# Two graph attention layers on one core: another order of the norm, the reciprocal and the row dots in layer 0

## The chip, the core and the metric

The kernel runs on one core of a Trainium2 chip. The core has a matrix engine (TensorE, PE in the profile, with its weight loads as PEld), a vector engine (VectorE, DVE), a scalar engine (ScalarE, ACT), GpSimd (POOL, which here issues the gathers and scatters) and SyncE (SP, which issues plain transfers). Each engine works through its own queue of instructions and waits on semaphores that other engines raise. Data lie in HBM, in the on-chip SBUF (128 partitions) and in PSUM, which PE writes. The metric is device microseconds of one execution: the median of several timed runs, beside one execution under the profiler.

## What is computed

Two layers over 2708 nodes with 1024 features, and a sparse adjacency matrix (at most 40 neighbours a node). Each layer is an attention over the neighbours, a residual and a norm over the features. The change touches layer 0:

```python
def _L0_gnn_ref(x, adj, Wf, bf, Wg, bg, W, bW):
    f = x @ Wf + bf
    g = x @ Wg + bg
    e = jax.nn.relu(f @ g.T)
    scores = jnp.where(adj > 0, e, NEG)
    attention = jax.nn.softmax(scores, axis=1)
    x_W = x @ W + bW
    return attention @ x_W
...
x = _layernorm(x + _L0_gnn_ref(...), axis=-1)
x = _layernorm(x + _L1_gnn_ref(...), axis=-1)
```

`_layernorm` subtracts the mean and divides by the root of the variance plus 1e-5. Layer 1 has scores `leaky_relu(f1 + f2.T)` with two vectors f1 and f2, one number per node each.

## The kernel before

First the adjacency rows are turned into lists of up to 40 neighbours, and nodes are sorted by degree into 85 groups of 32. Four groups make a block of 128 rows (block 0 has one group). A tile is one gather of 128 rows of x: four neighbours for each of the 32 nodes of a group. The blocks of layer 0 have 20 tiles, but for the first two (15 and 3) and the last three (16, 16, 15).

The weights are joined beforehand: M = Wf Wgᵀ, so the score of node n with neighbour m is x[n] M x[m] plus a term q. Layer 0's loop `for k, u in enumerate(units)` has 22 steps, in the order of blocks 1, 0, 2, 3 and so on. Every step holds work of several blocks at once:

- `lay.sums` (PE): the sums of block u, with weights st on the rows gathered in `ring` (20 slots). It also makes `totals`, the softmax denominators, by small matmuls into a PSUM tile pt. As its matmuls finish, slots become free, and POOL issues the next gathers into them. DVE takes the reciprocal ri of the totals, and ACT writes y, the scaled sums.
- `x_turn` (PE, ACT): transposes of the block two steps ahead, xb to xT, through two pt tiles (the pool ps_t has two buffers, which totals, q_spread and y's transposes share).
- `product(.., Wt, 1)`: the block behind times W, into a pm tile (the pool ps_m has two buffers). `f_product`: the block ahead times M, also into a pm tile. `turn(y..)` transposes y for the next step.
- `replicate(b, r)` (ACT): copies group r of F, 32 rows of pm, four times into the 128 partitions of Fr[b, r]. Four such copies are one replica.
- `dots` (DVE): for each tile of the next block, one fused multiply and sum of ring rows with Fr over 1024 features, into one column of scores. The tiles of groups 0 and 1 come first, alternating, then those of 2 and 3.
- `soft` (DVE, one Exp on ACT): the softmax over the block's scores; it makes st for the next step's sums, and last the row sums rs.
- `close(back)`, a generator: adds the residual z (gathered by `load_residual`) to the product in pm, runs `norm`, writes X1S for layer 1, computes two row dots with u2b and u1b (f2 and f1 of layer 1), and scatters z with the dots into table T1. The tile zs is the only buffer of z.
- `q_dot`, `q_spread`: the q term of a block, one dot over xb and a small matmul.
- `load_x`, `load_lists`: POOL's gathers of xb and of four parts of the neighbour lists SL.

`norm` is bn_stats and bn_aggr on DVE, then a root by an integer first guess and three Newton turns of three instructions each, then one Identity on ACT with scale and bias. Both layers use it.

All five engines are wrapped in `InOrder`, so each engine's instructions run in the order in which the Python code issues them. Nearly all show line 71, that of the wrapper, in the profile, so groups are told apart by their tiles. The order on DVE in one step of the loop is: add, bn_stats, root and sh of `close`; q dot; the row dots; ri; the dots; q; softmax. On ACT it is: Exp, y's transposes copied, replica 0, Identity on z, replicas 1 and 2, y, xT, replica 3. On POOL: ring gathers, scatter into T1, xb, z, four list gathers.

Of the kernel before, what the change touches and what calls it, by code (L numbers as in the profile page):

```python
# [8 lines left out]
F32 = mybir.dt.float32  # L9
BF16 = mybir.dt.bfloat16  # L10
I32 = mybir.dt.int32
AF = mybir.ActivationFunctionType
ALU = mybir.AluOpType
# [5 lines left out]
EPS = 1e-5  # L19
# [87 lines left out]
def listed_path(ctx, tc, x, adj, Wf, bf, Wg, bg, W, bW, W1, a1, a2, out):  # L107
# [491 lines left out]
    def scatter(table, idx, src):  # L599
        pool.indirect_dma_start(  # L600
            out=table, out_offset=bass.IndirectOffsetOnAxis(ap=idx, axis=0), in_=src,
            in_offset=None, bounds_check=N - 1, oob_is_err=False)

    def norm(z, n, made=None):


        st = small.tile([P, H, 6], F32, name="bst")
        mv = small.tile([P, 2], F32, name="mv")
        for h in range(H):
            if made is not None:  # L610
                made(h)
            dve.bn_stats(st[:n, h, :], z[:n, h * 512:(h + 1) * 512])
        dve.bn_aggr(mv[:n], st[:n])
        var, r, t = (small.tile([P, 1], F32, name=s) for s in ("var", "rstd", "newton"))
        dve.tensor_scalar(var[:n], mv[:n, 1:2], EPS, None, op0=ALU.add)
        ri, ti = r.bitcast(I32), t.bitcast(I32)
        dve.tensor_scalar(ti[:n], var.bitcast(I32)[:n], 1, None, op0=ALU.logical_shift_right)
        dve.tensor_scalar(ri[:n], ti[:n], -1.0, float(0x5F3759DF), op0=ALU.mult, op1=ALU.add)
        for _ in range(3):
            dve.tensor_scalar(t[:n], var[:n], r[:n], r[:n], op0=ALU.mult, op1=ALU.mult)  # L620
            dve.tensor_scalar(t[:n], t[:n], -0.5, 1.5, op0=ALU.mult, op1=ALU.add)
            dve.tensor_scalar(r[:n], r[:n], t[:n], None, op0=ALU.mult)
        sh = small.tile([P, 1], F32, name="sh")
        dve.tensor_scalar(sh[:n], mv[:n, 0:1], r[:n], -1.0, op0=ALU.mult, op1=ALU.mult)
        yield
        act.activation(z[:n, :D], z[:n, :D], AF.Identity, bias=sh[:n], scale=r[:n])
# [24 lines left out]
    class Layer:  # L651
# [57 lines left out]
            u.rs = small.tile([P, Q], F32, name="rs")  # L709
            dve.tensor_reduce(u.rs[:, :u.G], sc, AX.X, ALU.add)  # L710

        def sums(self, u, po, y):

            place = lambda k, h: 32 * ((k + 2 * h) % 4)

            def totals():
                pt = ps_t.tile([P, 4, P], F32, name="pt")  # L720
                for h in range(H):
                    for k in range(u.G):
                        j = place(k, h)
                        pe.matmul(pt[j:j + 32, 0, h:h + 1], stack, u.rs[:, k:k + 1], start=True, stop=True)
                return pt

            index = {(k, t): m for m, (k, g, t) in enumerate(u.tiles)}

            queues = []
            for c in range(4):  # L730
                two = [(k, h) for h, k in enumerate((c, (c + 2) % 4)) if k < u.G]
                if c > 1:
                    two.reverse()
                queues.append([(k, h, t) for t in range(u.T) for k, h in two if t < TILES[u.gs[k]]])
            done, halves, pt = 0, {}, None
            while any(queues):
                if pt is None and done >= min(4, u.T):
                    pt = totals()
                now = [q.pop(0) for q in queues if q]
                for k, h, t in now:  # L740
                    j = place(k, h)
                    pe.matmul(po[j:j + 32, h, :], u.st[:, u.col[k, t], :],
                              self.rows(u.at + index[k, t])[:, h * 512:(h + 1) * 512],
                              start=(t == 0), stop=(t == TILES[u.gs[k]] - 1))
                for k, h, t in now:
                    halves[k, t] = halves.get((k, t), 0) + 1
                    if halves[k, t] == H:
                        self.free.add(u.at + index[k, t])
                        self.gathers()
                        done += 1  # L750
            if pt is None:
                pt = totals()
            ri = small.tile([P, H], F32, name="ri")
            spans = [(slice(0, P), slice(0, H))] if u.G == 4 else \
                [(slice(j, j + 32), slice(h, h + 1)) for h in range(H) for j in (place(0, h),)]
            for rows, h in spans:
                dve.reciprocal(ri[rows, h], pt[rows, 0, h])
            for h in range(H):
                rows = slice(0, P) if u.G == 4 else slice(place(0, h), place(0, h) + 32)
                c = slice(h * 512, (h + 1) * 512)  # L760
                act.activation(y[rows, c], po[rows, h, :], AF.Copy, scale=ri[rows, h:h + 1])
# [95 lines left out]
    def load_lists(b):  # L857
        for g in groups[b]:
            gather(pool, SL[:, g, :], LD[:, :], idq[:, g:g + 1], N * Q)
# [9 lines left out]
    with ExitStack() as s0s:  # L869
# [10 lines left out]
        def load_x(b):  # L880
            xb[b] = xp.tile([P, D], F32, name="xb") if b > 0 else zs[:, :D]
            gather(pool, xb[b][:nrows[b]], x, ids[:nrows[b], b:b + 1])
# [5 lines left out]
        def q_dot(b):  # L888
            n = nrows[b]
            qs = small.tile([P, 1], F32, name="qs")  # L890
            dot(xb[b][:n], rb, n, qs[:n])
            qd[b] = spread(qs[:n], n, "qd")
# [9 lines left out]
        def x_turn(b):  # L902
            xTs[b] = tp.tile([P, KC, P], F32, name="xT")
            for _ in turn(xb[b], nrows[b], xTs[b]):
                pass
# [4 lines left out]
        def replicate(b, k):  # L910

            Fr[b, k] = frp.tile([P, D], F32, name="Fr")
            for p in range(Q):
                act.copy(Fr[b, k][32 * p:32 * p + 32, :], flat(F[b])[32 * k:32 * k + 32, :])

        def dots(u, lo, hi):
            for m in range(lo, hi):
                k, g, t = u.tiles[m]
                dot(lay.rows(u.at + m), Fr[u.b, k], P, u.sc[:, k, t:t + 1])
# [12 lines left out]
        def close(b):  # L932

            n, m, z = nrows[b], valid[b], Z.pop(b)
            pm = Wp.pop(b)

            def add(h):
                c = slice(h * 512, (h + 1) * 512)
                dve.tensor_add(z[:n, c], pm[h][:n, h, :], z[:n, c])

            if b + 1 < NB:
                dve.tensor_add(z[:n, :D], flat(pm)[:n], z[:n, :D])
            steps = norm(z, n, None if b + 1 < NB else add)
            next(steps)
            yield
            for _ in steps:
                pass
            sp.dma_start(X1S[start[b]:start[b] + m, :], z[:m, :D])
            yield
            dot(z[:n, :D], u2b, n, z[:n, D:D + 1])  # L950
            dot(z[:n, :D], u1b, n, f1[:n, b:b + 1])
            yield
            if z is not zs:
                pool.memset(z[:, D + 1:], 0.0)
            scatter(T1[:, :], ids[:m, b:b + 1], z[:m])
# [65 lines left out]
        soft(units[0])  # L1021
        for _ in spread2:
            pass
        closing, loaded = iter(()), 3
        for k, u in enumerate(units):
            nxt = units[k + 1] if k + 1 < len(units) else None
            b = u.b
# [6 lines left out]
            if back is not None:  # L1034
                for _ in yTs[back][1]:
                    pass
            reps = list(range(len(nxt.gs))) if nxt is not None and not first else []
            for r in reps[:1]:
                replicate(nxt.b, r)
            next(closing, None)  # L1040
            if loaded is not None:
                q_dot(loaded)
                loaded = None
            next(closing, None)
            for r in reps[1:3]:
                replicate(nxt.b, r)
            if nxt is None:

                for _ in closing:
                    pass  # L1050
                Wp[back] = product(P, yTs.pop(back)[0], Wt, 1)
            lay.sums(u, po, y[b])
            for _ in closing:
                pass
            closing = iter(())
            if ahead is not None and not first:
                x_turn(ahead)
            if k + 3 < NB and not first:
                loaded = seq[k + 3]
                load_x(loaded)  # L1060
            if back is not None and nxt is not None:
                load_residual(back)
                if back > 0:
                    Wp[back] = product(P, yTs.pop(back)[0], Wt, 1)
                else:
                    Wp[back] = whole(split_product(yTs.pop(back)[0], Wt, frp.tile([P, D], F32, name="Fr"), 1))
# [16 lines left out]
            if k + 2 == NB:  # L1083
                for _ in steps:
                    pass
            if k + 4 < NB and not first:
                load_lists(seq[k + 4])
            if nxt is not None:
                dots(nxt, 0, len(nxt.tiles))
            for _ in spreading:  # L1090
                pass
            if nxt is not None:
                soft(nxt)
            if back is not None:
                closing = close(back)
                next(closing)
# [529 lines left out]
```

## Time and profile before

| What | Value |
|---|---|
| median of 3 timed runs | 1904.17 us (1901.87 to 1906.42) |
| profiled execution | 1750.29 us, span 1748.6 us |
| mean granted PE clock in it | 0.957 |
| PE, DVE, ACT, POOL busy, of the span | 1563.6, 1297.5, 643.5, 1180.9 us |
| same, 0 to 220 us (lists, weights) | 171.5, 171.7, 109.6, 164.9 us |
| same, 220 to 326 us (layer 0, first two blocks) | 89.2, 66.0, 44.5, 67.2 us |
| same, 326 to 977 us (16 steps of layer 0's loop) | 630.0, 594.9, 333.2, 454.8 us |
| same, 977 to 1130 us (layer 0's end) | 138.5, 117.2, 67.9, 65.3 us |
| same, 1130 to 1748.6 us (layer 1) | 534.6, 347.6, 88.3, 428.7 us |

The profile is of one execution; its busy times are sums of instruction durations of one engine. A matmul's end is modelled, so PE's busy time is a rough figure. A wait is named after what released the engine last. The timed runs are executions without the profiler, and their median lies 154 us above the profiled one.

### The profile page before, as it was taken

To read this page: it belongs to the slowest core of one execution; us is meant where nothing else is said; L and a number is where in the kernel's file an instruction comes from. 1 tells how busy PE (TensorE), PEld (TensorE's weight loads), DVE (VectorE), ACT (ScalarE), POOL (GpSimd) and SP (SyncE) were. 2 spreads that over 40 slices of the span, in tenths; PEclk is the share of its full clock that TensorE was granted. 3 is DMA by queue.
4 is the path that set the end of the run, shared out by engine and by line. 5 is a ranking of instruction groups with operands and counts; after the bars stand their busy time and mean duration, and the time that the engine had idled before them with its cause. 6 is when DMAs were issued, how large, how long until landed. Compare 5 with 4: busy or idle time off the path is not lost. (4 is left out here: it accounts for less than half of the span.)

```text
span 1748.6 us, 23112 instructions
## 1 busy us (share of the span) xinstructions
PE 1563.6 (89%) x6969; PEld 675.5 (39%) x6969; DVE 1297.5 (74%) x4262; ACT 643.5 (37%) x902; POOL 1180.9 (68%) x1195
## 2 busy tenths in 40 slices
PE   4999578899999999999999999559899888999896
PEld 2444233344444444444444444213344333343332
DVE  5879846899999989998999977547465555665652
ACT  4555455444444554555554444101111111111111
POOL 7888476467667767776677743177777777777740
PEclk8999778999999999999999999879999999999998
DMA  7656168578877777888887876399999999999960
GB/s 287 228 185 236 38 232 309 199 252 292 302 277 283 269 253 276 294 293 284 303 299 285 291 267 249 121 394 357 367 374 392 391 397 375 384 392 390 396 253 38
DMA packets 149986, 502.80 MB, mean 288 GB/s; under 512 B 32340, under 2 KB 32372, under 8 KB 147144
## 3 DMA queue, kind: packets, MB, share of 16 engines
q0 software_dynamic: 132032, 428.29, 66.2%
q1 hardware_dynamic: 10202, 55.72, 8.4%
q10 hardware_dynamic: 7618, 17.23, 2.7%
q8 instruction: 57, 0.93, 0.2%
q14 instruction: 77, 0.63, 0.1%
HBM read 509.64 MB, written 33.75 MB: 311 GB/s over the span
## 5 line engine op out<-in xcount | busy, mean ns | idle before, releaser
L71 POOL DMA_INDIRECT ring<-in_x_dram,SL x405 | 429.9, 1062 | 164.0 <-issue 70.0
L71 DVE SCALAR_TENSOR_TENSOR j<-ring,Fr 128x1024 bf16<-128x1024 f32 x402 | 493.9, 1229 | 41.1 <-DMA ring<-in_x_dram,SL 13.9
L71 PE MATMUL po<-ring,st 128*32 128x512 f32 x2616 | 324.4, 616 | 56.9 <-ACT y L71 32.5
L71 ACT COPY Fr<-pm 32x1024 f32<-32x1024 f32 (+2 forms) x353 | 340.6, 965 | 18.8 <-PE pm L71 14.1
L71 PE MATMUL pm<-M,yT 128*128 128x512 f32 (+1 forms) x704 | 313.3, 598 | 0.5 <-ACT yT L71 0.5
L71 PE MATMUL pm<-Wt,xT 128*128 128x512 f32 (+1 forms) x704 | 300.5, 599 | 4.7 <-DMA Wt<-in_L_gnn_W_dram 4.7
L71 POOL DMA_INDIRECT ring<-T,SL x249 | 247.0, 992 | 80.5 <-issue 66.3
L71 PE MATMUL pm<-M,xT 128*128 128x512 f32 x672 | 297.5, 601 | 0.0
L71 ACT ACTIVATE scores<-scores 128x12 f32<-128x12 f32 (+9 forms) x65 | 14.0, 216 | 631.6 <-DVE scores L71 631.6
L71 PEld LDWEIGHTS pm<-M,yT 128*128 128x128 f32 (+1 forms) x704 | 127.8, 186 | 185.0 <-issue 183.8
L71 PEld LDWEIGHTS pm<-Wt,xT 128*128 128x128 f32 (+1 forms) x704 | 131.0, 189 | 163.4 <-issue 154.6
L71 PEld LDWEIGHTS pm<-M,xT 128*128 128x128 f32 x672 | 130.2, 194 | 158.0 <-issue 155.1
L71 POOL DMA_INDIRECT more<-T,SL x156 | 154.6, 991 | 48.5 <-issue 43.8
L71 PEld LDWEIGHTS po<-ring,st 128*32 128x32 f32 x2616 | 95.9, 113 | 229.8 <-issue 174.0
L412 POOL TENSOR_TENSOR adj<-adj,iota 128x2708 f32<-128x2708 f32 (+3 forms) x23 | 130.6, 5685 | 22.7 <-ACT adj L71 22.6
L415 DVE MAX8 cand<-adj 128x8 f32<-128x136 f32 (+2 forms) x440 | 97.2, 285 | 37.4 <-POOL adj L412 37.4
L71 PE MATMUL pm<-halfT,WfT 128*128 128x512 f32 x256 | 114.1, 601 | 1.1 <-ACT WfT L71 1.1
L71 POOL DMA_INDIRECT SL<-LD,idq x85 | 86.4, 1016 | 25.8 <-issue 24.0
L71 PE MATMUL po<-more,st 128*32 128x512 f32 x624 | 82.4, 625 | 14.3 <-ACT y L71 14.3
L71 DVE TENSOR_SCALAR scores<-ring,f1q 128x4 f32<-128x4 f32 (+6 forms) x69 | 16.5, 245 | 104.1 <-DMA ring<-T,SL 93.1
L71 POOL DMA_INDIRECT z<-in_x_dram,ids x21 | 24.0, 1142 | 87.1 <-DVE j L71 36.4
L71 PEld LDWEIGHTS pm<-halfT,WfT 128*128 128x128 f32 x256 | 48.2, 193 | 58.0 <-issue 55.2
(214 smaller groups left out, 1539.5 us busy)
## 6 DMA issues: line engine op xcount, KB each, us to landing
adj<-in_adj_dram SPq DMA_DIRECT2D x21, 1354.0 KB, 5.8
X1S<-z SPq DMA_DIRECT2D x19, 512.0 KB, 5.2
ring<-in_x_dram,SL POOLq DMA_INDIRECT x405, 6.5
rows<-in_L_gnn_Wg_dram ACTq DMA_DIRECT2D x8, 512.0 KB, 4.4
rows<-in_L_gnn_Wf_dram ACTq DMA_DIRECT2D x8, 512.0 KB, 3.5
rows<-in_L_gnn_W_dram ACTq DMA_DIRECT2D x8, 512.0 KB, 6.1
Wt<-in_L_gnn_W_dram ACTq DMA_DIRECT2D x1, 4096.0 KB
M<-in_L_gnn_W_dram SPq DMA_DIRECT2D x1, 4096.0 KB
```

Of the source, the lines that this page charges most:

```text
L71: made = self.tc.keep_in_program_order(op(*args, **kwargs))
L412: nc.gpsimd.tensor_tensor(k[:n, cut], k[:n, cut], iota[:n, cut], op=ALU.mult)
L415: nc.vector.max(cand[:n, s, :], k[:n, s * SEG:min((s + 1) * SEG, N)])
```

## The change

In layer 0 `close` no longer calls `norm`, except for the last block. The residual add becomes a fused instruction that also sums the row; the mean is one more small instruction; ACT squares z with the mean as bias and sums (its elementwise output goes into the pm tile, where nobody reads it); the root is a new helper `rsqrt`, with Newton turns of two instructions instead of three, which `norm` uses too, in both layers. The generator has more stops, so that its parts lie elsewhere in the step: the square ahead of replica 0, the root, Identity and the rest inside `sums` by a callback `aside` after the totals. The reciprocal ri is taken right after the totals. Five dots of the next block follow at once, ahead of the two row dots; the last four dots come after q. The q dot moves from after the norm to the end of the step before. The list gathers are issued ahead of the residual gather.

```diff
+    def rsqrt(v, n, scale):
+        half, r, t = (small.tile([P, 1], F32, name=s) for s in ("half", "rstd", "newton"))
+        dve.tensor_scalar(half[:n], v, 0.5 * scale, 0.5 * EPS, op0=ALU.mult, op1=ALU.add)
+        ri, ti = r.bitcast(I32), t.bitcast(I32)
+        dve.tensor_scalar(ti[:n], half.bitcast(I32)[:n], 1, None, op0=ALU.logical_shift_right)
+        dve.tensor_scalar(ri[:n], ti[:n], -1.0, float(0x5F3759DF - 0x400000 - (1 << 31)), op0=ALU.mult, op1=ALU.add)
+        for _ in range(3):
+            dve.tensor_scalar(t[:n], half[:n], r[:n], r[:n], op0=ALU.mult, op1=ALU.mult)
+            dve.tensor_scalar(r[:n], t[:n], 1.5, r[:n], op0=ALU.subtract, op1=ALU.mult)
+        return r
...
-        var, r, t = (small.tile([P, 1], F32, name=s) for s in ("var", "rstd", "newton"))
-        dve.tensor_scalar(var[:n], mv[:n, 1:2], EPS, None, op0=ALU.add)
...
-        for _ in range(3):
-            dve.tensor_scalar(t[:n], var[:n], r[:n], r[:n], op0=ALU.mult, op1=ALU.mult)
-            dve.tensor_scalar(t[:n], t[:n], -0.5, 1.5, op0=ALU.mult, op1=ALU.add)
-            dve.tensor_scalar(r[:n], r[:n], t[:n], None, op0=ALU.mult)
+        r = rsqrt(mv[:n, 1:2], n, 1.0)
...
-        def sums(self, u, po, y):
+        def sums(self, u, po, y, aside):
...
             def totals():
...
-                return pt
+                for rows, h in spans:
+                    dve.reciprocal(ri[rows, h], pt[rows, 0, h])
+                aside()
...
-            for rows, h in spans:
-                dve.reciprocal(ri[rows, h], pt[rows, 0, h])
...
             if b + 1 < NB:
-                dve.tensor_add(z[:n, :D], flat(pm)[:n], z[:n, :D])
-            steps = norm(z, n, None if b + 1 < NB else add)
-            next(steps)
-            yield
-            for _ in steps:
-                pass
+                mean, ss, sh = (small.tile([P, 1], F32, name=s) for s in ("mean", "ss", "sh"))
+                dve.scalar_tensor_tensor(z[:n, :D], flat(pm)[:n], 1.0, z[:n, :D], op0=ALU.mult, op1=ALU.add,
+                                         accum_out=mean[:n])
+                dve.tensor_scalar(mean[:n], mean[:n], -1.0 / D, None, op0=ALU.mult)
+                yield
+                act.activation(flat(pm)[:n], z[:n, :D], AF.Square, bias=mean[:n], accum_out=ss[:n])
+                yield
+                r = rsqrt(ss[:n], n, 1.0 / D)
+                dve.tensor_scalar(sh[:n], mean[:n], r[:n], None, op0=ALU.mult)
+                yield
+                act.activation(z[:n, :D], z[:n, :D], AF.Identity, bias=sh[:n], scale=r[:n])
...
-        closing, loaded = iter(()), 3
+        closing = iter(())
+        q_dot(3)
         for k, u in enumerate(units):
...
+            next(closing, None)
             for r in reps[:1]:
                 replicate(nxt.b, r)
-            next(closing, None)
-            if loaded is not None:
-                q_dot(loaded)
-                loaded = None
-            next(closing, None)
-            for r in reps[1:3]:
-                replicate(nxt.b, r)
...
-            lay.sums(u, po, y[b])
+            def aside():
+                next(closing, None)
+                for r in reps[1:2]:
+                    replicate(nxt.b, r)
+                next(closing, None)
+                for r in reps[2:3]:
+                    replicate(nxt.b, r)
+
+            lay.sums(u, po, y[b], aside)
+            early = 0
+            if nxt is not None and not first:
+                early = min(5, sum(k < 2 for k, _, _ in nxt.tiles))
+                dots(nxt, 0, early)
             for _ in closing:
                 pass
...
                 load_x(loaded)
+            if k + 4 < NB and not first:
+                load_lists(seq[k + 4])
             if back is not None and nxt is not None:
                 load_residual(back)
...
-            if k + 4 < NB and not first:
-                load_lists(seq[k + 4])
             if nxt is not None:
-                dots(nxt, 0, len(nxt.tiles))
+                dots(nxt, early, max(0, len(nxt.tiles) - 4))
             for _ in spreading:
                 pass
             if nxt is not None:
+                dots(nxt, max(0, len(nxt.tiles) - 4), len(nxt.tiles))
                 soft(nxt)
+            if loaded is not None:
+                q_dot(loaded)
+                loaded = None
```

More of the change, by code (lines that the diff above doesn't have):

```diff
@@ L613, in norm @@
         dve.bn_aggr(mv[:n], st[:n])
-        var, r, t = (small.tile([P, 1], F32, name=s) for s in ("var", "rstd", "newton"))
-        dve.tensor_scalar(var[:n], mv[:n, 1:2], EPS, None, op0=ALU.add)
-        ri, ti = r.bitcast(I32), t.bitcast(I32)
-        dve.tensor_scalar(ti[:n], var.bitcast(I32)[:n], 1, None, op0=ALU.logical_shift_right)
-        dve.tensor_scalar(ri[:n], ti[:n], -1.0, float(0x5F3759DF), op0=ALU.mult, op1=ALU.add)
-        for _ in range(3):
-            dve.tensor_scalar(t[:n], var[:n], r[:n], r[:n], op0=ALU.mult, op1=ALU.mult)
-            dve.tensor_scalar(t[:n], t[:n], -0.5, 1.5, op0=ALU.mult, op1=ALU.add)
-            dve.tensor_scalar(r[:n], r[:n], t[:n], None, op0=ALU.mult)
+        r = rsqrt(mv[:n, 1:2], n, 1.0)
         sh = small.tile([P, 1], F32, name="sh")
@@ L710, in soft @@
             dve.tensor_reduce(u.rs[:, :u.G], sc, AX.X, ALU.add)
-        def sums(self, u, po, y):
+        def sums(self, u, po, y, aside):
             place = lambda k, h: 32 * ((k + 2 * h) % 4)
+            ri = small.tile([P, H], F32, name="ri")
             def totals():
@@ L724, in totals @@
                         pe.matmul(pt[j:j + 32, 0, h:h + 1], stack, u.rs[:, k:k + 1], start=True, stop=True)
-                return pt
+                spans = [(slice(0, P), slice(0, H))] if u.G == 4 else \
+                    [(slice(j, j + 32), slice(h, h + 1)) for h in range(H) for j in (place(0, h),)]
+                for rows, h in spans:
+                    dve.reciprocal(ri[rows, h], pt[rows, 0, h])
+                aside()
             index = {(k, t): m for m, (k, g, t) in enumerate(u.tiles)}
@@ L734, in sums @@
                 queues.append([(k, h, t) for t in range(u.T) for k, h in two if t < TILES[u.gs[k]]])
-            done, halves, pt = 0, {}, None
+            done, halves, summed = 0, {}, False
             while any(queues):
-                if pt is None and done >= min(4, u.T):
-                    pt = totals()
+                if not summed and done >= min(4, u.T):
+                    summed = True
+                    totals()
                 now = [q.pop(0) for q in queues if q]
@@ L750, in sums @@
                         done += 1
[L751 to L755, printed above, removed]
-            for rows, h in spans:
-                dve.reciprocal(ri[rows, h], pt[rows, 0, h])
+            if not summed:
+                totals()
             for h in range(H):
@@ L941, in close @@
             if b + 1 < NB:
-                dve.tensor_add(z[:n, :D], flat(pm)[:n], z[:n, :D])
-            steps = norm(z, n, None if b + 1 < NB else add)
-            next(steps)
-            yield
-            for _ in steps:
-                pass
+                mean, ss, sh = (small.tile([P, 1], F32, name=s) for s in ("mean", "ss", "sh"))
[9 more added lines that the diff above has]
+                act.activation(z[:n, :D], z[:n, :D], AF.Identity, bias=sh[:n], scale=r[:n])
+            else:
+                steps = norm(z, n, add)
+                next(steps)
+                yield
+                yield
+                yield
+                for _ in steps:
+                    pass
             sp.dma_start(X1S[start[b]:start[b] + m, :], z[:m, :D])
@@ L1092, in listed_path @@
             if nxt is not None:
+                dots(nxt, max(0, len(nxt.tiles) - 4), len(nxt.tiles))
                 soft(nxt)
+            if loaded is not None:
+                q_dot(loaded)
+                loaded = None
             if back is not None:
```

## The prediction

> **What bounds the kernel now.** I read the stretches first. Between 326 and 977 us, sixteen equal steps of layer 0's loop run; PE is busy 630 of 651 us and DVE 595, all other engines far less. So both are near full, and I asked which waits for which. PE's waits from 300 to 1120 us:
>
> ```profile
> PE pt L71 <- DVE ri L71: 13.7, 14, 3.1
> PE po L71 <- DVE st L71: 5.4, 9, 1.0
> PE pm L71 <- ACT Fr L71: 5.3, 2, 4.1
> ```
>
> (us in total, times, longest.) PE waits for DVE, at two places: the second transpose group of xb waits for the reciprocal ri, and the sums wait for the weights st. Then the timeline of DVE for one step, the one from 609.74 us (start, us, engine, line, operation, idle before):
>
> ```profile
> 609.74 0.17 DVE L71 TENSOR_REDUCE rs<-scores 128x4 f32<-128x24 f32 x1
> 610.33 1.23 DVE L71 TENSOR_TENSOR z<-pm,z 128x1024 f32<-128x1024 f32 x1 [0.42 <-DMA z<-in_x_dram,ids]
> ...
> 615.96 0.21 DVE L71 TENSOR_SCALAR sh<-mv,rstd 128x1 f32<-128x1 f32 x1
> 616.09 1.21 DVE L71 SCALAR_TENSOR_TENSOR j<-xb,rb 128x1024 bf16<-128x1024 f32 x1
> ...
> 617.48 1.22 DVE L71 SCALAR_TENSOR_TENSOR j<-z,u2b 128x1024 bf16<-128x1024 f32 x1
> ...
> 619.90 0.17 DVE L71 RECIPROCAL ri<-pt 128x2 f32<-128x2 f32 x1
> 620.02 1.23 DVE L71 SCALAR_TENSOR_TENSOR j<-ring,Fr 128x1024 bf16<-128x1024 f32 x1
> ...
> 621.55 1.22 DVE L71 SCALAR_TENSOR_TENSOR j<-ring,Fr 128x1024 bf16<-128x1024 f32 x1 [0.30 <-ACT Fr L71]
> ...
> 650.64 0.17 DVE L71 TENSOR_REDUCE rs<-scores 128x4 f32<-128x24 f32 x1
> ```
>
> From rs to rs is 40.90 us. DVE is never idle over 0.8 us in it: norm, q dot, two row dots, ri, twenty dots, softmax. The second dot starts 11.81 us after rs, and waits 0.30 us for ACT's copies of F. And ACT in the same step:
>
> ```profile
> 609.93 4.04 ACT L71 COPY Fr<-pm 32x1024 f32<-32x1024 f32 x4
> 616.20 1.24 ACT L71 ACTIVATE z<-z,sh,rstd 128x1024 f32<-128x1024 f32 x1 [2.23 <-DVE sh L71]
> 617.47 8.13 ACT L71 COPY Fr<-pm 32x1024 f32<-32x1024 f32 x8
> ```
>
> The first replica Fr is copied while DVE computes the norm; the second ends at 621.54, and the second dot starts at 621.55. The replicas are thus only just hidden. All of DVE's norm and row dots (10.2 us) lie in a stretch in which the dots couldn't run anyway.
>
> PE's own floor: steps in which it waits for nothing start their sums at 367.73, 406.94 and 446.25, so 39.2 to 39.3 us. The sixteen steps from 326.40 to 976.85 take 650.45, or 40.65 each. All that could be won from PE's waits there is 16 x 1.4 = 22 us.
>
> **What the Trainium skill says.** "Perfetto Trace Analysis", section "Tensor Engine Instruction (MATMUL, LD_WEIGHTS)": ACT, DVE and GpSimd queues are strict FIFO. The trace agrees: ACT idles 2.23 us ahead of the z instruction while the copies behind it could have run. "ScalarE: Activation LUTs", section "Step-by-step: what each stage is for": writing PSUM is quicker for ScalarE than writing SBUF; no row here has SBUF to PSUM. "TensorE: Matmul & The Clock Gate", section "Part 1: The HAM clock gate": idle PE loses its clock. Here a 3.14 us gap before 1027.44 is followed by a product of 14.72 instead of 13.90 us and transposes and bias row 0.9 us longer: 1.7 us.
>
> **The change part by part**, over DVE's step, T = start of rs. DVE's new order is rs, q dot, add, mean, ri, root, five dots, two row dots, eleven dots, q, four dots, softmax; ACT's is Square, two replicas (8 copies), z, one replica, y, xT, one replica.
>
> 1. q dot, 0.09 to 1.48 (the old start-to-start: 616.09 to 617.48). z's gather has landed by then: it was 0.42 us late against T + 0.6.
> 2. Summing add: 1.26, as a dot row with its accumulator read starts the next; to 2.74. mean 0.15; to 2.89. ri (0.17) and the totals' matmuls, which end 1.8 after T, are done in time. PE's wait for ri goes: -13.7 us of PE.
> 3. Square on ACT: not in the trace. Above: 1.24 like z's Identity (SBUF to SBUF); below: 1.01, the 128x1024 copy out of PSUM. I take 1.24, since the source is SBUF, and add the accumulator read of adj's rows, 0.19. From 2.93 to 4.36.
> 4. Shorter root: three small rows at 0.19 start to start, three pairs of 0.31 + 0.25, sh 0.21: 2.46 us, where the old had 2.8 + 0.2. It starts at 4.40 and ends at 6.86. Bn_stats and its aggregate (1.53) are gone. DVE's work per step falls by some 1.9 us.
> 5. But the replicas stand behind Square in ACT's queue. Eight copies at 8.13: first replica at 8.42, second at 12.49. Tiles alternate between groups 0 and 1, so dot 0 runs at 8.45 and dot 1 at 12.52. DVE idles 1.4 (Square), 1.6 and 2.8 us. Before, dot 1 ran at 11.81.
> 6. After that nineteen dots, 19 x 1.265 = 24.04; the row dots, now behind five dots, 2.54; q 0.14; softmax 3.99 (605.75 to 609.74). 12.52 + 24.04 + 2.54 + 0.14 + 3.99 = 43.23. Before: 11.81 + 24.04 + 0.14 + 3.99 = 39.98, and 0.92 of small ring waits make the 40.90.
>
> So the row dots were free under the replicas, and now they are not; the idle they leave is filled with waiting.
>
> 7. Lists ahead of z: POOL's z gather waited 4.33 us for T's scatter, and four list gathers of 1.30 start to start, 5.2 us, fit there. z is issued some 1 us later at most, hidden by the q dot. Ring gathers start 3 us sooner; 20 x 1.30 from T + 1 keeps ahead of the dots, so the 0.92 of ring waits goes. It is in step 6 already. xb, ahead of the lists, is unmoved and has landed (5.4 us after issue).
> SP's X1S store goes out 6 us later with z (13.7 instead of 7.7 after T); it lands 5.2 later and only the next z gather needs it. T's scatter waits for the row dots, done at T + 20.1; ring gathers hold POOL until T + 27 anyway.
> 8. q four dots earlier frees a PSUM buffer for y's transposes: nothing, PE isn't waiting there.
> 9. pm is held by Square until T + 4.4; PE wants it 10 us after T: nothing. The fourth replica ends at 24.3, PE's F product starts at 25.1: just hidden.
> 10. PE then has 39.25 of work in 43.23, and a gap of 4 us before each sums. By the 1.7 us above, its slower clock takes half of that; DVE still ends last.
> 11. Shorter root in layer 1: 0.56 us for each of 22 blocks on DVE, behind gathers (DMA share 0.91 over that stretch): nothing, but on the two ends, layer 0's last norm and the last norm of all: -1.1.
>
> Sum: 16 x (43.23 - 40.65) = +41.3. The next two steps have 16 tiles: DVE 43.23 - 4 x 1.265 = 38.2, PE bound. They took 39.65 and 42.52 (with the 3.14 wait and its clock). Now 39.25 + 2.0 for the clock, and 42.52 - 3.14 - 1.7 = 37.7: together -3.2. The last step, with PE busy throughout, is equal. +41.3 - 3.2 - 1.1 = +37. Profiled time 1750.29 (span 1748.6): 1787. The median of the runs shown is 154 us above the profile, for which I see no cause in the trace. I take it as constant: 1904 + 37 = 1941.
>
> **Rivals.**
> A. DVE and PE as forecast, but PE's clock in the timed runs is what makes them 154 us longer than the profile. If PE's step is over 43.2 (clock below 39.25 / 43.2 = 0.91 of the profiled one), the longer DVE step is covered. For it: the 154 us; against: the granted clock over 326 to 977 us is 0.99. ri is then early enough either way: no change, 1904.
> B. The other side: faster. Place: DVE's stretch from T to dot 1. If that falls from 12.5 to below 8.5, DVE fits PE's 39.25 and PE's waits of 22 us go: 1904 - 22 - 1 = 1881. It decides from 4 us less, so two replicas would have to be out by the time I have one. For it: ACT is only 51% busy there. Against: the FIFO and the 8.13.
> C. Slower still: PE's gap cools it by more than 4 us, as after 346 us where a 4.08 gap was followed by a product of 15.86, and sums too run slow (9.62 for 7.05 at 328): 2.4 + 2.6 = 5.0, a step of 44.3. 16 x 1.1 = 17 more: 1958.
>
> **How the numbers follow.** Forecast 0.68, A 0.09, B 0.11, C 0.12. The forecast's own range: Square 0.43 shorter (write to PSUM, read hidden) is 7 us less, 0.5 us per step of unseen semaphore time or ri held up by slow totals 8 more, clock after the 16 tile steps 2 either way: 1928 to 1954. The whole range takes in C and stops short of B: 1902 to 1960. A measurement of this kernel tells 0.2%, 3.8 us, from no change. Slower: 0.68 + 0.12 + 0.02 of A; same: 0.07; faster 0.11.
>
> **What would show it.** Right: in the stretch 326 to 1000 DVE's rs recur every 43 us; dot 1 follows rs by 12.5, ended by ACT Fr; waits of DVE on Square near 1.4 each; PE's wait for ri gone and its wait for st up from 5.4 to over 20 us; ring waits of dots near zero; layer 1 equal in length. Wrong: rs every 39 to 40 us, or PE busy throughout (A, B); Square over 2 us; a step set by PE with its products at 15 us or more (C).

## The result, and the profile after

| | before | after |
|---|---|---|
| median of 4 timed runs of one job | 1905.3 us (1901.87 to 1909.23) | 1987.61 us (1975.87 to 2006.42) |
| ratio, 95% interval | | 1.0425 [1.0372, 1.0479] |
| profiled execution (span), clock | 1750.29 us (1748.6), 0.957 | 1975.87 us (1973.8), 0.924 |

By the medians the change costs 82 us where 37 were forecast, and the time lies above the whole range of the forecast, which ended at 1960. The two profiled executions must not be subtracted. Jobs, sets of runs made together, ran on different chips: the kernel before takes 1747 to 1749 us on two of them (profiled there: 1742.6) and 1888 to 1910 on three others (profiled: 1904.3). Which chip the first job's runs had is not on record, but its profile of before fits the quick ones and its median the late ones. So the 154 us between the two lie between chips, and not between runs with and without a profiler. Below they are called quick and late chips, and ratios are taken within one job only. On the late chips the runs of one kernel spread by up to 4%, and the comparisons below leave out those over 1.5% above the fastest of their kernel. Each late chip was met in one job only, so a chip and what else went on at that time can't be told apart.

The traces differ too. Those of quick chips, the first profile of before among them, hold 21,672 to 21,837 semaphore events, those of late chips, the profile after among them, 9,737 to 12,172. What ended a wait is read from these events. So in a trace of a late chip `issue` or `remote` can stand for an event that is missing from it.

DVE's timeline in the profile after, one step (start, us, engine, line, operation, idle before):

```profile
641.05 0.17 DVE L71 TENSOR_REDUCE rs<-scores 128x4 f32<-128x24 f32 x1
...
645.26 0.15 DVE L71 TENSOR_SCALAR half<-ss 128x1 f32<-128x1 f32 x1 [0.82 <-ACT pm L71]
...
649.19 1.23 DVE L71 SCALAR_TENSOR_TENSOR j<-ring,Fr 128x1024 bf16<-128x1024 f32 x1 [1.48 <-issue]
...
653.26 1.23 DVE L71 SCALAR_TENSOR_TENSOR j<-ring,Fr 128x1024 bf16<-128x1024 f32 x1 [2.84 <-issue]
...
681.46 0.22 DVE L71 TENSOR_SCALAR q<-pt,s 128x4 f32<-128x4 f32 x1 [6.34 <-remote]
...
690.30 0.17 DVE L71 TENSOR_REDUCE rs<-scores 128x4 f32<-128x24 f32 x1
```

The first half is as forecast: dot 1, the second of the twenty, starts 12.2 us after rs (forecast 12.52), after DVE idled 0.8, 1.5 and 2.8. The second half is not: DVE stands 6.34 us at q, and the step takes 49.25 us instead of 43.2. ACT in the same step:

```profile
643.98 1.12 ACT L71 ACTIVATE pm<-z,mean 128x1024 f32<-128x1024 f32 x1 [2.61 <-DVE mean L71]
...
645.13 8.09 ACT L71 COPY Fr<-pm 32x1024 f32<-32x1024 f32 x8
653.25 1.24 ACT L71 ACTIVATE z<-z,sh,rstd 128x1024 f32<-128x1024 f32 x1
```

The eight copies run only after Square, as the forecast had it. DVE's waits from 300 to 1330 us (us in total, times, longest us), some left out:

```profile
DVE j L71 <- ACT Fr L71: 55.6, 16, 19.3
DVE q L71 <- remote: 51.8, 9, 8.1
...
DVE ri L71 <- PE po L71: 38.3, 14, 8.6
```

The forecast had nothing for DVE's waits at q and at ri. PE, over the same stretch:

```profile
PE pm L71 <- issue: 44.6, 48, 2.6
PE po L71 <- DVE st L71: 41.0, 13, 5.8
```

PE waits for the weights st, as forecast (5.4 before, "over 20" expected), but it also stands idle 48 times ahead of a matmul into pm, mostly inside its products, without a named releaser; the first profile of before showed none of these. Below they are called holes.

### The profile page after: what moved, and what is told of

The parts are those of the page before. It is cut to its first block, busy times and chain, and to the rows that moved or that the text cites. A ratio compares the mean times of both kernels' runs of the same rounds, so it can differ in the third digit from the quotient of the medians.

```text
span 1973.8 us, 22931 instructions
## 1 busy us (share of the span) xinstructions
PE 1644.7 (83%) x6947; PEld 691.1 (35%) x6969; DVE 1237.4 (63%) x4109; ACT 675.4 (34%) x944; POOL 1167.1 (59%) x1195
## 5 line engine op out<-in xcount | busy, mean ns | idle before, releaser
L71 POOL DMA_INDIRECT ring<-in_x_dram,SL x405 | 417.3, 1030 | 374.2 <-PE po L71 232.4
L71 PE MATMUL po<-ring,st 128*32 128x512 f32 x2616 | 358.6, 652 | 116.5 <-issue 57.2
L71 PE MATMUL pm<-M,xT 128*128 128x512 f32 x672 | 312.4, 618 | 23.7 <-issue 23.7
L71 PE MATMUL pm<-Wt,xT 128*128 128x512 f32 (+1 forms) x704 | 308.4, 601 | 16.4 <-issue 15.1
L71 PE MATMUL pm<-M,yT 128*128 128x512 f32 (+1 forms) x704 | 318.1, 601 | 4.0 <-issue 2.3
L71 PEld LDWEIGHTS po<-ring,st 128*32 128x32 f32 x2616 | 102.0, 118 | 308.1 <-issue 256.6
L71 ACT ACTIVATE y<-po,ri 128x512 f32<-128x512 f32 (+1 forms) x88 | 58.1, 685 | 255.6 <-remote 129.4
L71 PE MATMUL po<-more,st 128*32 128x512 f32 x624 | 98.8, 658 | 21.1 <-issue 20.6
L71 PE MATMUL pt<-ident,y 128*128 128x128 f32 (+1 forms) x352 | 52.7, 273 | 23.4 <-issue 19.7
L71 ACT COPY xT<-pt 128x512 f32<-128x512 f32 (+2 forms) x109 | 48.2, 499 | 63.2 <-PE pt L71 48.0
```

The costliest lines, as they stand in the source:

```text
L71: made = self.tc.keep_in_program_order(op(*args, **kwargs))
```

## Experiments

**1. The two kernels on several chips.** The kernel before is c_before and b2_before, the changed one the other four.

> The kernel before, once more, with its profile taken among the timed runs. Theory 1 (the 154 us between the profiled execution and the timed ones are work that the profile of before didn't show, such as PE slowed or held up): the span of this profile is near 1900 us, with gaps of PE and a clock below 0.957. Theory 2 (a constant outside the span): span near 1749 us again, and a time near 1905.

> The changed kernel once more, on a chip where the kernel before takes about 1747 us. Theory FIFO (DVE's step grows to 43.2 us, by the sum of the prediction): 1747 + 37 = 1784 us, ratio 1.021, rs every 43.2 us from the third to the eighteenth block, PE's records free of holes of a microsecond and more inside a product. Rival (the change is slow by 4% on any chip, since PE's releases come late in it): ratio 1.035 or more, with DVE's q waiting 3 to 8 us for PE as in the first profile.

> The kernel before. If it takes about 1905 us here, its profile shows what the 158 us against 1747 are. Theory L (on such a chip PE's releases reach the others late): DVE's waits for PE are many in it, and records of PE have holes inside products; layer 1, which the change hardly touches, is longer than the 605 us of the run at 1741. Rival (transfers are slower there): DVE's waits are for gathers, and GB/s in layer 1 are lower without holes in PE.

> The changed kernel. Where before takes 1747 us: theory FIFO 1784 us (ratio 1.021) with rs every 43.2 us; rival, that it is slow by 4% anywhere, ratio 1.035 or more. Where before takes 1905 us: 1.04 to 1.05 again.

> The changed kernel. Where before takes about 1747 us: theory FIFO says rs every 43.2 us over sixteen steps and 1784 us (ratio 1.021). Rival (PE is held up by the changed order itself, on any chip): holes of PE without a releaser as on the other chips, steps of 49 us, ratio 1.035 or more. Where before takes about 1900 us: 1.03 to 1.05 as measured before.

> The changed kernel again, to stand beside the other three on one chip. If PE is late here as on the chips of the earlier jobs, 1.03 to 1.05 of before, with steps from rs to rs of 43 us where DVE finds PE's results done and of 49 us where it doesn't. If this is a chip on which before takes about 1750 us, the forecast's sum should hold: +37 us, 1.021, with steps of 43.2 us throughout.

| run | chip | this, us | before in the job, us | ratio |
|---|---|---|---|---|
| before, c | quick | 1747.68 | 1747.09 | 1.0002 [0.9988, 1.0016] |
| after, a4 | quick | 1779.76 | 1749.09 | 1.0188 [1.014, 1.0235] |
| before, b2 | late | 1901.34 | 1887.99 | 1.0068 [1.0008, 1.0128] |
| after, a2 | late (that of b2) | 1947.86 | 1887.99 | 1.0323 [1.0255, 1.0391] |
| after, c | late | 1979.4 (2 runs) | 1900.9 | none given |
| after, a3 | late | 1965.7 (2 runs) | 1901.5 | none given |

On a quick chip the change costs 30.7 us; on the late ones about 60 to 78, and in the result's job 82, or 72 without its longest run. So the chip decides whether the forecast's 37 holds. (The same source as before came out 0.7% off on b2's chip from two runs, so differences below 1% there say little.) The timeline of DVE in a4:

```profile
665.76 0.17 DVE L71 TENSOR_REDUCE rs<-scores 128x4 f32<-128x24 f32 x1
...
673.90 1.23 DVE L71 SCALAR_TENSOR_TENSOR j<-ring,Fr 128x1024 bf16<-128x1024 f32 x1 [1.47 <-ACT Fr L71]
...
677.97 1.23 DVE L71 SCALAR_TENSOR_TENSOR j<-ring,Fr 128x1024 bf16<-128x1024 f32 x1 [2.84 <-ACT Fr L71]
...
699.76 0.21 DVE L71 TENSOR_SCALAR q<-pt,s 128x4 f32<-128x4 f32 x1
...
708.84 0.17 DVE L71 TENSOR_REDUCE rs<-scores 128x4 f32<-128x24 f32 x1
```

43.08 us from rs to rs against 43.23 forecast; no wait at q; and ACT's copies named as the releaser of both dots. All sixteen steps take 42.7 to 43.1. On b2's chip, the stretches of the sixteen steps of before and of after (columns: the stretch and its length; busy us of PE, PEld, DVE, ACT, POOL; granted clock; DMA share; GB/s):

```profile
341.00:1049.00 708.00, 660.50 (x2924) 286.80 (x2924) 597.20 (x1324) 334.24 (x404) 472.89 (x431) 0.97 0.75 260
```

```profile
329.00:1097.00 768.00, 673.15 (x2935) 284.06 (x2937) 568.41 (x1263) 353.63 (x435) 440.09 (x432) 0.93 0.68 240
```

The loop alone is 60 us longer, which is the whole of the difference between these two profiles; PE's recorded work grew by 13 of them, and PE is idle in the rest. In c_before, on a quick chip, the same sixteen steps of before took 653 us, and b2's extra 54 lie in two places. Some 30 are in its first four steps (340.77 to 535.06), over which the granted clock was 0.89, against 0.99 in c_before. The other 24 are in the later twelve, where the clock was 1.00 in both. There the sums differ, while the products are equal and without holes; first b2_before (535.06 to 1048.48), then c_before (483.59 to 972.53); columns: count, busy us, mean ns of one, idle us before:

```profile
L71 PE MATMUL pm<-Wt,xT 128*128 128x512 f32 x384 | 166.8, 592 | 0.0
L71 PE MATMUL po<-ring,st 128*32 128x512 f32 x960 | 129.5, 602 | 19.5 <-DVE st L71 13.0 <-issue 4.3
```

```profile
L71 PE MATMUL pm<-Wt,xT 128*128 128x512 f32 x384 | 166.8, 592 | 0.0
L71 PE MATMUL po<-ring,st 128*32 128x512 f32 x960 | 107.2, 594 | 5.8 <-DVE st L71 5.8
```

In a2 the products have holes, as in the profile after. PE's timeline there, with the product that starts at 590.27:

```profile
589.70 0.28 PE L71 MATMUL pt<-qd,rep 128*128 128x4 f32 x2
...
598.30 0.59 PE L71 MATMUL pm<-M,xT 128*128 128x512 f32 x1 [0.58 <-issue]
600.41 0.59 PE L71 MATMUL pm<-M,xT 128*128 128x512 f32 x1 [1.52 <-issue]
602.51 1.01 PE L71 MATMUL pm<-M,xT 128*128 128x512 f32 x1 [1.51 <-issue]
```

and DVE there:

```profile
604.72 0.22 DVE L71 TENSOR_SCALAR q<-pt,s 128x4 f32<-128x4 f32 x1 [6.30 <-remote]
```

q needs the two matmuls recorded at 589.70, yet is released only at 604.72, 15 us later, and after holes in the product behind them. In the semaphore events of a4 the signal follows the recorded end by 0.01 us (691.47, 691.48); in a2 it comes at 604.69, after an end recorded at 589.98.

**2. The replica ahead of Square.** The forecast's mechanism by itself.

```diff
-            next(closing, None)
             for r in reps[:1]:
                 replicate(nxt.b, r)
+            next(closing, None)
```

> The changed kernel with ACT's Square put behind the first replica instead of ahead of it. Theory FIFO (the replicas held up behind Square set the step): first replica back at T + 4.3, second at T + 9.8 instead of 12.5, so 2.7 us less on each of 16 steps: 1988 - 43 = 1945 us. Rival (PE held up or slowed is what makes the changed kernel slow, whatever ACT's order): within 10 us of 1988.

> The changed kernel with the first replica ahead of Square. It took 1744 us (0.997) where before takes 1747. Where before takes about 1900 us: theory FIFO alone says 40 us less than the changed kernel in the same job; theory L (q ahead of the last four dots waits for a late PE) says q's waits of 46 us or more stay, so it is still slower than before, ratio 1.01 to 1.03.

On a quick chip 0.9971 [0.9944, 0.9998], against 1.0188 for the changed kernel on another: most steps take 40.3 us instead of 42.9. What DVE waits for there, 300 to 1240 us:

```profile
DVE half L71 <- ACT pm L71: 56.3, 21, 3.7
...
DVE j L71 <- ACT Fr L71: 9.2, 19, 0.6
```

The waits for Fr are gone but for 0.5 us each; DVE waits 2.7 us for Square instead, together 3.2 us a step, where a4's step has 0.9, 1.5 and 2.8. This is the strict queue that the Trainium skill states ("Perfetto Trace Analysis", "Tensor Engine Instruction (MATMUL, LD_WEIGHTS)"), with its price measured: two lines swapped in ACT's queue, 2.6 us a step. On a late chip it took 1947 to 1966 us, and the two runs of a3 in the same job 1951 and 1980, so what the swap is worth there isn't resolved. The loss stays: the ratio to before is 1.0274 [1.0182, 1.0367].

**3. bn_stats in place of Square.** Summing add and Square go, the old norm comes back with the shorter root; the rest of the change stays.

```diff
-                act.activation(flat(pm)[:n], z[:n, :D], AF.Square, bias=mean[:n], accum_out=ss[:n])
...
+                dve.tensor_add(z[:n, :D], flat(pm)[:n], z[:n, :D])
+            steps = norm(z, n, None if b + 1 < NB else add)
```

> The changed kernel with the statistics back on DVE (bn_stats and bn_aggr), no Square; all else of the change stays. Theory FIFO: ACT's replicas no longer wait, dots start at T + 6.8 and go on at T + 8.3; the DVE step is about 39.1 us, PE's 39.25 is the bound, faster than before by 16 x 1.4 + 5 = 27 us: 1878 us (ratio 0.986). Rival (the moved row dots and the q ahead of the last four dots cost by themselves): slower than before, 1930 us or more.

> The changed kernel with bn_stats on DVE instead of Square on ACT, as before; it had ratio 0.991 where before takes 1747 us. Where before takes 1905 us: theory FIFO alone would give the same 0.99; theory L adds q's waits, so ratio 1.00 to 1.02.

On a quick chip 0.9906 [0.9881, 0.9931]: dot 1 comes 8.4 us after rs, against 11.7 in c_before. On b2's chip 0.9985 [0.9943, 1.0027], better than either expectation. Its sixteen steps there:

```profile
341.00:1042.00 701.00, 647.63 (x2925) 277.82 (x2924) 589.03 (x1275) 332.75 (x400) 457.94 (x432) 0.96 0.74 262
```

So with DVE busier than in a2 (589 against 568 us) the loop is 67 us shorter. And although q and ri keep their early places, DVE's waits from 329 to 1100 us fall at q to 9.7 us (2 times) and at ri on po to 5.7 (2 times), from 43.8 and 36.6 in a2. By these two profiles PE's lateness isn't a constant of the chip but grows with the arrangement around it.

**4. q behind all dots**, as before; Square and the rest as changed.

```diff
-                dots(nxt, early, max(0, len(nxt.tiles) - 4))
+                dots(nxt, early, len(nxt.tiles))
             for _ in spreading:
                 pass
             if nxt is not None:
-                dots(nxt, max(0, len(nxt.tiles) - 4), len(nxt.tiles))
                 soft(nxt)
```

> The changed kernel with q put back behind all dots of the next block. Where before takes 1747 us: no change against the changed kernel (within 4 us). Where it takes 1905 us, theory L (q, moved ahead of four dots, makes DVE wait for a late PE): DVE's waits at q, 52 and 76 us in the two profiles, shrink by up to 5 us each, so 30 to 50 us less than the changed kernel. Rival (PE itself is late, and DVE waits for it at ri or st instead): within 10 us of the changed kernel.

On b2's chip 1905 to 1921 us, ratio 1.0138 [1.0079, 1.0197], where a2 has 1.0323; by the medians 31 us below a2. DVE's waits from 329 to 1100 us:

```profile
DVE ri L71 <- PE po L71: 44.2, 13, 11.5
...
DVE q L71 <- remote: 10.7, 7, 2.6
```

The step can be added up. In the profile after, q is released 40.4 us after rs (641.05 to 681.46), and from q on there follow four dots and the softmax, 8.84 us: 49.25. With q behind the dots only the softmax follows, 4.1 by the forecast's rows: 44.5, and the median of this run's sixteen steps is 44.55. The two numbers come from two chips, and DVE waits at q in only 7 of the steps, so their agreement supports this and doesn't prove it. The wait at ri stays.

**5. Both places mended, on the late chip of a3.** First bn_stats with q last, then the replica ahead of Square with q last.

> bn_stats on DVE and q behind all dots; the rest of the change stays. Where before takes 1747 us: as with q ahead, 1734 us (within 4). Where before takes about 1900 us: theory L says q's remaining waits of 10 us go, ratio 0.990 to 0.997. Rival (PE sets the step there, whatever DVE waits for): 0.9985 again, within 0.003.

> The changed kernel with both mended: first replica ahead of Square, q behind all dots. Where before takes 1747 us: 1744 us (within 4), as with the replica alone. Where before takes about 1900 us: if FIFO and L are all of the loss, ratio 0.995 to 1.005; rival (the early reciprocal, whose waits for PE were 45 us, costs by itself): 1.01 or more.

1.0229 [1.0138, 1.032] and 1.0174 [1.0096, 1.0252]. The second is 17 us below e1_again, which is the worth of q's place there, but slower than before; DVE still waits 34.7 us at ri. The first missed its expectation (0.990 to 0.997) and contradicts itself: its profiled run, the shortest, took 1916.08 us with a loop of 709, the others up to 1958.26. I take no size from it, but it stands against reading e2_again as a cure on every late chip.

**6. The reciprocal late.** It is taken behind the program of sums and the root; q last too.

```diff
-                for rows, h in spans:
-                    dve.reciprocal(ri[rows, h], pt[rows, 0, h])
                 aside()
+                return pt
...
+            for rows, h in spans:
+                dve.reciprocal(ri[rows, h], pt[rows, 0, h])
```

> The changed kernel with both of DVE's waits for PE put back where before has them: q behind all the dots, and the reciprocal behind the sums' program and the root. Square and the queue of replicas stay as changed. Theory (DVE, put ahead of a late PE, waits at q and at ri, and that is all that the forecast lacked): DVE's waits at ri go from about 44 us to under 10 and the ratio falls from q last's 1.014 towards what the forecast's step alone gives where PE is the slower one: 1.00 to 1.01. Rival (the reciprocal is only where the lateness shows; with it late, DVE waits at the next thing that it needs of PE): equal to q last's 1.01 to 1.02.

> The changed kernel with q and the reciprocal both late, again. In the last job, with PE never late, it equalled the changed kernel (1.019 both), as it should. If before takes about 1900 us here: theory (the two early waits of DVE for a late PE are what the forecast lacked) 1.00 to 1.01, waits at ri under 10 us; rival (the lateness shows at DVE's next need of PE) 1.014 or more, as with q alone last. If before takes about 1750 us: 1.019 again, and the question stays open.

> The same, and bn_stats on DVE in place of Square, so that the replicas leave ACT early too: of the change there remain the shorter root, the lists, five dots ahead of the row dots and four dots behind the spreading. Theory: nothing that costs is left, so no slower than before: 0.985 to 1.00. Rival (another part, the dots ahead or the lists, costs where PE is late): 1.01 to 1.02.

All three fell on a quick chip, that of a4: 1.0191 [1.0148, 1.0234] and 1.0177 [1.0158, 1.0197], equal to a4's 1.0188. There neither place costs anything, just as the forecast said of q. With bn_stats instead of Square 0.9922 [0.9897, 0.9947]. What the early reciprocal costs on a late chip was not measured.

**7. Two parts alone: shorter root and lists ahead, on the kernel before.**

```diff
-        var, r, t = (small.tile([P, 1], F32, name=s) for s in ("var", "rstd", "newton"))
...
+        r = rsqrt(mv[:n, 1:2], n, 1.0)
...
                 load_x(loaded)
+            if k + 4 < NB and not first:
+                load_lists(seq[k + 4])
```

> The kernel before with two parts of the change alone: the shorter root and the lists ahead of the residual. By the forecast's terms: 0.56 us of DVE less in each step, in a stretch in which DVE then waits for replicas (nothing), 0.9 us of ring waits per step gone: 0.99 to 1.00 of before. Rival (the list gathers hold up z's gather and with it the add): 1.00 to 1.01.

> The kernel before with the shorter root and the lists ahead, again. In the last job, where before took 1749 us, it took 0.992 of it, by steps of 40.0 instead of 40.8 us. If before takes about 1900 us here, PE is the later one in most steps, and what DVE saves in its stretch up to the second dot (0.8 us of ring waits per step) is covered for the most part: 0.99 to 1.00. Rival (lists that hold up z's gather cost where the engines are late): 1.00 to 1.01.

0.9918 [0.989, 0.9945] and 0.9923 [0.9905, 0.9942]: a little faster than before, twice, on one quick chip. DVE's waits in the first of them, 300 to 1240 us:

```profile
DVE z L71 <- DMA z<-in_x_dram,ids: 19.0, 17, 5.5
...
DVE j L71 <- DMA ring<-in_x_dram,SL: 4.5, 9, 1.4
```

In c_before these were 13.4 and 14.4: the ring waits fall by 10 us, and the waits for z's gather grow by 6. In the second run they were 21.0 and 10.4. The sixteen steps take 640 us (319.5 to 959.4, from rs to rs) against 653 in c_before; in the second run's profile, which is of the longest of its executions (1744.03 us), 650. This version beats both kernels where it was run; on a late chip it wasn't run.

## Why the forecast was right in direction and wrong in size

Against a4, whose chip is like that of the profile it was worked from:

- Step 1 (q dot): add at 1.48 us after rs, as written.
- Step 2: mean at 2.74, as written; ri waits 0.26 us there, under Square. "Done in time" holds on a quick chip only: in the profile after DVE waited 38.3 us at ri.
- Step 3 (Square): 1.12 us, not 1.24; with its read, DVE goes on at 4.21 instead of 4.40. The Trainium skill ("ScalarE: Activation LUTs", "Step-by-step: what each stage is for") calls PSUM the quicker destination, and the trace fits: 1.12 into PSUM, 1.24 for Identity into SBUF, both from SBUF, though the two differ in their function too. The forecast took its upper bound against what the page says.
- Step 4 (root): 2.46 us forecast, 2.46 measured (669.97 to 672.43).
- Step 5 (the queue on ACT): dot 0 at 8.14, dot 1 at 12.21 (8.45, 12.52): the error of step 3 carried on. e1 shows the cause by taking it away.
- Step 6: 43.08 for this step, 42.9 on average.
- Step 7 (lists): a4's dots wait 1.5 us for the ring, once, between 300 and 1240. Right, and experiment 7 fits: with the root, and without the rest of the change, it is a gain.
- Step 9 (pm, the fourth replica): PE's waits on Fr are 6.9 us in a4 against 5.3. Right.
- Step 10: PE waits for st 40.2 us over 15 steps in a4, 2.7 each and not 4; DVE ends last. Right there.
- Step 11 (layer 1): from layer 1's first scores to the end c_before takes 604.8 us, a4 606.6. Nothing, within 2 us.
- Sum: +37 forecast, +30.7 measured on a quick chip. The dots' term was 16 x 2.58; against c_before (653.3 us for sixteen steps, 40.83 each) and 42.9 it is 33. The range of 1928 to 1954 doesn't come out of its terms: 7 and 2 below, 8 and 2 above give 1932 to 1951.

The step that failed is the last sentence: "The median of the runs shown is 154 us above the profile, for which I see no cause in the trace. I take it as constant". It isn't a constant that can be added. On a late chip PE and its signals come late in the loop too (708 us for sixteen steps in b2, 650 in the profile before), and the change, which makes DVE wait for PE at new places, costs more there: 60 us on b2's chip against 30.7 on a4's. Step 8 ("q four dots earlier ... nothing, PE isn't waiting there") looked only at whether PE waits for DVE and not at whether DVE would wait for PE. On b2's chip q's place alone, beside Square, is worth some 31 of the 60 us; on a3's chip, with the replica mended, 17.

The shares don't add up: with bn_stats in place of Square (e2_again) the whole loss goes on b2's chip, though q stays early. One reading is that Square and the late replicas make st late, that DVE's early needs of PE make it wait in the same step, and that PE then waits for st. It is not shown, and one number stands against it: PE waits longer for st in e2_again, where nothing is lost, than in a2 (30.7 and 25.3 us, from 329 to 1100). What goes with the loss is rather PE's holes ahead of matmuls into pm, from 300 to 1240 us: 39 to 57 us in the five late traces with Square that were read over that stretch (a2, a3, e1_again, e3, e6), 22 to 25 in the three without (b2, e2_again, e5).

Rival A supposed that a slow PE would cover the longer DVE step, and said that ri is early enough either way; every late chip shows the opposite. Rival C (PE cooled by its gaps) isn't what happened on the quick chip: in a4 the products keep 13.9 us with PE's gaps present. On late chips it is open. There the loss lies more in holes than in longer matmuls, but the granted clock over the sixteen steps is 0.93 in a2 against 0.97 in b2, and no run separates the two. Rival B (dots sooner, a gain) is where e2_bn ends on a quick chip: dot 1 at 8.4 us, below the 8.5 that B asked for, and 0.4 us less a step than c_before. The change as a whole isn't there, since its second dot comes no sooner. (e8_root_lists gains 0.8 us a step in its first profile and 0.2 in its second, with dot 1 at 11.4, so not by B's way.)

What stays open: why PE's signals come late on some chips; why the kernels with Square have loops of 724 us and more there (e6; 729 in e3, 731 in e1_again, 768 and 772 in a2 and a3) and those without it 701 to 709 (e2_again, e5, and before), where Square's output into a pm tile, which PE's products use too, was never moved by itself; how much the reciprocal's place costs there; and the share of each in the job of the result, which had no single parts in it.

## What to carry to other kernels

An instruction that waits on another engine, moved ahead in a strict queue, costs nothing only as long as that engine is early; before moving it, add up the loop that runs through both engines (here st, sums, product, q, four dots, softmax, st) and ask how late the other may come. A part that moves work to an idle engine must be placed behind what that engine's next reader is waiting for: here a replica, and not the square, is what the dots wait for (e1, on a quick chip). When a profile and the timed runs differ by 8%, the profile is of another balance between the engines, and a sum made on it needs the second balance as a rival with a loss, not only with cover.

## What the runs showed of the hardware

One and the same kernel takes 1747 us on some chips and 1888 to 1910 on others, with a granted clock of 0.964 and 0.935 in profiles of each.

On the late ones PE's semaphore signals can come long after the recorded end of their matmuls. In a2's loop those that release q come up to 16 us after it (1022.87 and 1038.84), in a4's loop within 0.02. They also come in bunches: in the profile after, five within 0.22 us (653.99 to 654.21) for matmuls with recorded ends from 648.90 to 650.36, told apart by their order.

What grows on a late chip depends on the kernel. In b2's later twelve steps, at full granted clock, the products are as in c_before and the sums take 129.5 us instead of 107.2. In a2 the products have holes: 41 us without a named releaser in the sixteen steps (24.0 ahead of matmuls with M, 17.4 with Wt), in a trace from which semaphore events are missing. b2 has 61 idle stretches of PE over 0.25 us of this kind after 300 us, 117.6 us together; 86 us of it lie ahead of sums, most of them in layer 1. c_before has none.

Layer 1, whose instructions the change hardly touches, is longer there as well: 683 us from its first scores in b2, 605 in c_before.
